# A two-layer graph attention kernel: the order of a few vector operations and of two loads

## The chip, the cores and the metric

The kernel runs on one core of a Trainium2 chip. A core has a TensorE (PE) for matrix products, a VectorE (DVE), a ScalarE (ACT) and a GpSimd (POOL) for the rest, and DMA queues that are fed here by SyncE (SP) and POOL. Every engine works through its own instructions in order and waits on semaphores for the others. The metric is the device time of one execution in microseconds (us), as the median of several.

## The reference

A graph attention network with two layers on 512 nodes of 768 features, then a residual sum and a layer norm:

```python
def gat_layer(x, W, a_s, a_d, b, edge_index, concat):
    n = x.shape[0]
    H, C = a_s.shape
    h = (x @ W).reshape(n, H, C)
    src, dst = (edge_index[0], edge_index[1])
    alpha_s = jnp.einsum('nhc,hc->nh', h, a_s)
    alpha_d = jnp.einsum('nhc,hc->nh', h, a_d)
    e = jax.nn.leaky_relu(alpha_s[src] + alpha_d[dst], NEG_SLOPE)
    m = jax.ops.segment_max(e, dst, num_segments=n)
    e = jnp.exp(e - m[dst])
    denom = jax.ops.segment_sum(e, dst, num_segments=n)
    alpha = e / (denom[dst] + EPS)
    msg = h[src] * alpha[:, :, None]
    out = jax.ops.segment_sum(msg, dst, num_segments=n)
    out = out.reshape(n, H * C) if concat else out.mean(axis=1)
    return out + b
...
h = gat_layer(x, W1, a_src1, a_dst1, b1, edge_list, concat=True)
h = jax.nn.elu(h)
out = gat_layer(h, W2, a_src2, a_dst2, b2, edge_list, concat=True)
...
x = _layernorm(x + _L0_gnn_ref(x, ...), axis=-1)
```

Layer 1 has 8 heads, each with a 768 x 768 slice of W1; layer 2 has one head, whose W2 has 8 x 768 rows. All data are float32. There are 16,896 edges with their self loops.

## The kernel before

The edges are turned once into a 512 x 512 matrix of counts (`cnt`, and `absent` where there is no edge), so that each head is dense: the features hs = x W1[h] (`projection`), the logits, the attention probabilities (`lift`, `leak`, `rank`, `weigh`, one block of 128 destinations each), their transpose PT, the aggregate of hs by PT with bias and elu (`mixed`, or `aggregate` and `elu`), whose transposed result gT is at once multiplied with W2's rows of this head (`second`) and added to layer 2's features h2. The loop over h (line 678) does the aggregate of head h, `second` of head h, the probabilities of head h + 1 and the projection of head h + 2. Layer 2 follows after the loop.

The three large products use a scheme of seven products of half matrices, P1 to P7, in the place of eight. It needs sums of quarters of both operands, which DVE makes: `left` (lines 228 to 231) of x or gT, `right` (L240, L241) of the weights, into t2 and t4, and for `mixed` `left_sums` (L586 to L589) of hs and `right_sums` (L597 to L600) of PT. A pair in `projection` or `second` is a multiplication on PE into a bank of PSUM and its evacuation by DVE or ACT; P2 adds to P1's bank, P4 to P7's and P3 to P5's, so PE may begin them only when the bank was evacuated. In `mixed` the products run P1, P6, P7, P2, P5, P4, P3 for three chunks c; P6 needs the second sum of PT (L598), P7 the third (L599), P4 the fourth (L600).

The program is written out by hand in the order in which each engine is to issue (`manual_schedule`); a planner doesn't reorder anything. Where a tile is used again, the framework adds the wait for the tile's last readers. Around the change:

- Head 1's projection runs over the start of the loop: `pairs[4]` to `pairs[13]`, each followed by the functions that `beside` lists for it. `give(t)` weighs a block of head 0's probabilities and sends it through DMA to be transposed (`turn_out`), `turn_in(t)` is an ACT copy of the landed block into PT (L553). `done[12]` and `pairs[13][1]` are the last two evacuations (L287). `some_logits` are two logit operations of head 1's block 2 (L257). `rsums` are the four sums of PT.
- `besides` goes to `mixed` of head 0 as the front of `fill`, a list of DVE operations with no hurry. `some(n)` issues n of them: one in the middle of each chunk, and at its end the rest of the list divided by the places still to come, rounded up.
- In the last turn of the loop (h = 6) the weight buffer "w2" gets W2's rows of head 7: a 576 KB piece into w2t1 (L103) and six row blocks of 384 KB (L109) from SP's queue, and from POOL's an adding transfer (L104), with a second one (L115, `last_sum`) later. Layer 2's vectors a_src2 and a_dst2, spread over 128 partitions, go into the buffers w2t2 and w2t4, which held the `right` sums of head 7's projection (L686). DVE multiplies W2's row blocks with them (L703, twelve operations into V), spread between the chunks c = 2 to 5 of head 6's aggregate, whose elu ends in L565.
- `second` evacuates P1 with L306 (L304 in head 0). `pairs[0][1]` and `pairs[1][1]` are the two halves of P1. `gsums[0]` to `gsums[3]` are gT's sums, L228 to L231. `spread` puts the logits of the next head through PE (L363), ahead of P2.

Of the kernel before, what the change touches and what calls it, by code (L numbers as in the profile page):

```python
# [36 lines left out]
def gat_pass(  # L37
# [19 lines left out]
    H = a_src1.shape[0]  # L57
# [40 lines left out]
    def load_w(W, h, slot, m):  # L98


        t1 = wpool.tile([P, HK, HALF], F32, name=f"{slot}t1")
        upper = m[:HK * P, :].rearrange("(k p) d -> p k d", p=P)
        nc.sync.dma_start(t1, upper[:, :, L])  # L103
        nc.gpsimd.dma_start(t1, upper[:, :, R], accum_op=ALU.add)  # L104
        W[h] = []
        for r in range(2):
            w = wpool.tile([P, HK, D], F32, name=f"{slot}{r}")
            for k in range(r * HK, (r + 1) * HK):
                nc.sync.dma_start(w[:, k - r * HK, :], m[k * P:(k + 1) * P, :])  # L109
            W[h].append(w)  # L110
        W[h].append(t1)

        def rest():

            nc.gpsimd.dma_start(W[h][0][:, :, R], m[HK * P:, R].rearrange("(k p) d -> p k d", p=P),  # L115
                                accum_op=ALU.add)
        return rest
# [4 lines left out]
    def load_w2(h, slot="w1"):  # L122
        return load_w(W2, h, slot, w2[h * D:(h + 1) * D, :])
# [99 lines left out]
    def left(aT, s):  # L223
        a11, a12 = aT[:, :HK, :HN], aT[:, HK:, :HN]
        a21, a22 = aT[:, :HK, HN:], aT[:, HK:, HN:]
        tt = nc.vector.tensor_tensor
        return dict(P1=a11, P2=a12, P3=s[:, 2], P4=a22, P5=s[:, 0], P6=s[:, 1], P7=a21), [
            lambda: tt(s[:, 0], a21, a22, op=ALU.subtract),  # L228
            lambda: tt(s[:, 1], s[:, 0], a11, op=ALU.subtract),
            lambda: tt(a21, a11, a21, op=ALU.subtract),  # L230
            lambda: tt(s[:, 2], a12, s[:, 1], op=ALU.add),  # L231
        ]
# [23 lines left out]
    def half_logits(h, t):  # L256
        return [lambda al=al, a=a, sign=sign: nc.vector.scalar_tensor_tensor(  # L257
            scr, HS[h][:, t, :], sign, a, op0=ALU.mult, op1=ALU.mult, accum_out=al[:, t:t + 1])
            for al, a, sign in zip(AL[h], A[h], (1.0, -1.0))]
# [138 lines left out]
    if not general:  # L398
# [5 lines left out]
        cps, done = {}, 0  # L404
# [49 lines left out]
        for n, batch in enumerate(batches):  # L454
# [9 lines left out]
            while pos < want:  # L464
                if pos == wholes:
                    pairs = projection(1, XA, B1)
# [19 lines left out]
    else:  # L486
# [16 lines left out]
        pairs = projection(1, XA, B1)  # L503
# [48 lines left out]
    def turn_in(t):  # L552
        nc.scalar.copy(PT.rearrange("p s n -> p (s n)").bitcast(U16).rearrange("p (s n h) -> p s n h", s=NT, h=2)[  # L553
            :, :, t * P:(t + 1) * P, :], parted.pop(t).rearrange("p (h s d) -> p s d h", h=2, s=NT))
# [24 lines left out]
    def left_sums(h):  # L579
        hs = HS[h]  # L580
        a11, a12, a21, a22 = hs[:, :2, L], hs[:, 2:, L], hs[:, :2, R], hs[:, 2:, R]
        s1, s2, s4 = (gS.rearrange("p a k n -> p a (k n)")[:, j, :].rearrange("p (k n) -> p k n", k=2)
                      for j in range(3))
        tt = nc.vector.tensor_tensor
        return dict(P1=a11, P2=a12, P3=s4, P4=a22, P5=s1, P6=s2, P7=a21), [
            lambda: tt(s1, a21, a22, op=ALU.subtract),  # L586
            lambda: tt(s2, s1, a11, op=ALU.subtract),
            lambda: tt(a21, a11, a21, op=ALU.subtract),
            lambda: tt(s4, a12, s2, op=ALU.add),  # L589
        ]  # L590
# [63 lines left out]
    AA, lsums = left_sums(0)  # L654
    BB, rsums = right_sums()
    some_logits = half_logits(1, 2)

    def give(t):
        weigh(q[t], t)
        turn_out(q[t], t)  # L660

    done = {n: (lambda n=n: pairs[n][1]()) for n in range(4, 13)}
    beside = {4: [lambda: give(0)], 5: [done[4]], 6: [done[5]], 7: [done[6], lambda: give(1)],
              8: [done[7], lambda: leak(q[3]), lambda: rank(q[3], 3), lambda: turn_in(0)], 9: [lambda: give(2), done[8]],
              10: [lambda: give(3), lambda: turn_in(1), done[9]], 11: [done[10], lsums[0]],
              12: [done[11], lambda: turn_in(2), *lsums[1:3]], 13: [done[12], some_logits[0], lambda: turn_in(3)]}
    for n in range(4, 14):
        pairs[n][0]()
        for f in beside[n]:
# [2 lines left out]
            load_w2(0)()  # L672
            B2, pending = right(W2[0], "w1")
    pairs[13][1]()
    for f in rsums:
        f()
    besides = [lsums[3], some_logits[1]]
    for h in range(H - 1):
        if h + 2 < H:
            load_w1(h + 2)()  # L680
        else:
            last_sum = load_w2(H - 1, "w2")
            A[H] = []
            for j, a in ((2, a_src2[0]), (4, a_dst2[0])):
                v = wpool.tile([P, HK, HALF], F32, name=f"w2t{j}").rearrange("p k n -> p (k n)")[:, :D]
                nc.sync.dma_start(v, row_bcast(a))  # L686
                A[H].append(v)
        GA, gsums = left(gT, gS)
        if h + 2 < H:
            finish = mixed(h, AA, BB, besides + [p for t in ((0, 1) if h else (0, 1, 3)) for p in half_logits(h + 1, t)])  # L690
        else:
            finish = []
            for c in range(DC):
                finish.append(aggregate(h, c))
                if c:
                    finish.pop(0)()
                if c < 2:
                    logits(h + 1, HS[h + 1], c)
                else:

                    for k in ((0, 1), (2,), (3,), (4, 5))[c - 2]:
                        for v, a, sign in zip(range(2), A[H], (1.0, -1.0)):
                            nc.vector.scalar_tensor_tensor(scr, W2[H - 1][k // HK][:, k % HK, :], sign, a,  # L703
                                                           op0=ALU.mult, op1=ALU.mult, accum_out=V[:, k, v:v + 1])
        besides = []
        if h + 2 < H:
            load_a(h + 2, a_src1[h + 2], a_dst1[h + 2])
        pairs = second(h, GA, B2)
        for m, _ in pairs[:2]:
            m()  # L710
        pairs[0][1]()
        for f in finish:
            f()
        gsums[0]()
        gsums[1]()
        pairs[1][1]()
        if pending:
            pending.pop(0)()
        spread(h + 1)
        pairs[2][0]()  # L720
        gsums[2]()
        pairs[3][0]()
        gsums[3]()
        if pending:
            pending.pop(0)()
        pairs[2][1]()
        pairs[3][1]()
        last = h + 2 == H
        q = [lift(h + 1, 0)]
        for n in range(2, 7):  # L730
            (m0, e0), (m1, e1) = pairs[2 * n:2 * n + 2]
            m0()
            if not last:
                m1()
            if n < 6:
                leak(q[n - 2])
                rank(q[n - 2], n - 2)
            if n < 5:
                q.append(lift(h + 1, n - 1))
            if last:  # L740

                if n > 3:
                    turn(q[n - 4], n - 4)
                if n == 6:
                    weigh(q[3], 3)
                m1(lambda: turn(q[3], 3) if n == 6 else None)
            if not last and n == 6:
                turn_in(0)
                weigh(q[2], 2)
                turn_out(q[2], 2)  # L750
            e0()
            if last and 2 < n < 6:
                weigh(q[n - 3], n - 3)
            if not last and 3 < n < 6:
                weigh(q[n - 4], n - 4)
                turn_out(q[n - 4], n - 4)
            if not last and n == 6:
                weigh(q[3], 3)
                turn_out(q[3], 3)
                load_w2(h + 1)()  # L760
            e1()
        if h + 2 < H:
            B_, sums = right(W1[h + 2], "w2")
            pairs = projection(h + 2, XA, B_)
            for n in range(14):
                pairs[n][0]()
                if n == 0:
                    turn_in(1)
                    B2, sums2 = right(W2[h + 1], "w1")
                if n in (1, 3):  # L770
                    sums[n // 2]()
                if n == 1:
                    AA, sums3 = left_sums(h + 1) if h + 3 < H else (None, [])
                pairs[n][1]()
                if n in (2, 4):
                    turn_in(1 + n // 2)
                if n == 5 and h + 3 < H:
                    BB, sums3 = right_sums()
                if 1 <= n < 9 and h + 3 < H:
                    sums3.pop(0)()  # L780
                if n in (9, 10):
                    sums2.pop(0)()
                if n in (11, 13):
                    logits(h + 2, HS[h + 2], 2 + (n - 11) // 2)
        else:
            last_sum()
            B2, sums2 = right(W2[H - 1], "w1")
# [35 lines left out]
    pairs = second(H - 1, GA, B2)  # L823
# [115 lines left out]
```

## Time and profile before

| | us |
|---|---|
| runs of the kernel before | 661.69, 660.57, 662.6; median 661.69 |
| the profiled execution, its own time | 662.61 |
| its span, first to last instruction | 660.8 |
| PE busy | 649.1 (98%) |
| DVE busy | 511.7 (77%) |
| ACT busy | 248.6 (38%) |
| POOL busy | 42.8 (6%) |
| DMA, mean over the span | 130 GB/s |

The page is of one execution. Times in the timeline are microseconds from the span's start: start, duration, engine, line, operation, output and inputs, shape, count; in brackets the idle time of the engine just before, and what ended it. Durations of neighbours overlap: a DVE operation starts before the one ahead of it is quite out of the pipe, so the distance from start to start is what an operation takes of its engine's time. On PE each product of `second` and `projection` is six instructions (1.94 us from start to start), each of `mixed` four (0.87 us).

### The profile page before, as it was taken

To read this page: it belongs to the slowest core of one execution; us is meant where nothing else is said; L and a number is where in the kernel's file an instruction comes from. 1 tells how busy PE (TensorE), PEld (TensorE's weight loads), DVE (VectorE), ACT (ScalarE), POOL (GpSimd) and SP (SyncE) were. 2 spreads that over 40 slices of the span, in tenths; PEclk is the share of its full clock that TensorE was granted. 3 is DMA by queue.
4 is the path that set the end of the run, shared out by engine and by line. 5 is a ranking of instruction groups with operands and counts; after the bars stand their busy time and mean duration, and the time that the engine had idled before them with its cause. 6 is when DMAs were issued, how large, how long until landed. Compare 5 with 4: busy or idle time off the path is not lost.

```text
span 660.8 us, 7107 instructions
## 1 busy us (share of the span) xinstructions
PE 649.1 (98%) x2419; PEld 401.1 (61%) x2419; DVE 511.7 (77%) x1102; ACT 248.6 (38%) x417; POOL 42.8 (6%) x52
## 2 busy tenths in 40 slices
PE   8999999999999999999999999999999999999995
PEld 4555567556865577556855586557755544644553
DVE  6979989977779587767688687868785579866785
ACT  2222646350635135440725035430735042333440
POOL 1300011010100110010000110011000000000000
PEclk9999999999999999999999999999999999999998
DMA  8801299177803882087605790196506674000122
GB/s 308 239 1 49 33 277 285 28 220 160 225 1 68 246 236 64 16 248 189 160 0 129 185 273 26 33 264 202 116 0 194 158 225 132 24 0 1 28 61 76
DMA packets 71355, 85.58 MB, mean 130 GB/s; under 512 B 36566, under 2 KB 55950, under 8 KB 71310
## 3 DMA queue, kind: packets, MB, share of 16 engines
q1 hardware_dynamic: 59022, 66.76, 32.2%
q0 software_dynamic: 12000, 17.70, 15.8%
q10 hardware_dynamic: 288, 0.59, 0.3%
q8 instruction: 21, 0.34, 0.2%
q14 instruction: 24, 0.20, 0.1%
HBM read 75.07 MB, written 1.57 MB: 116 GB/s over the span
## 4 chain that ended last, share of the span: by engine, by line
PE 93%; DMA 3%; DVE 2%; issue 1%; SPq 0%; ACT 0%; DVEq 0%
PE mm L248 61%; PE mm L625 17%; PE mm L352 5%; PE mm L571 3%; PE mm L891 3%; PE tr L430 2%; DMA w2t<-in_L_gnn_a_dst_dram 2%; DMA hs<-in_x_dram 1%; DVE scr L703 1%; PE bc L430 1%; PE bc L363 0%; DVE gT L565 0%; PE mm L327 0%; PE tr L819 0%; PE tr L540 0%
## 5 line engine op out<-in xcount | busy, mean ns | idle before, releaser
L248 PE MATMUL mm<-w,gT 128*128 128x384 f32 x288 | 97.8, 488 | 1.4 <-DVE u L306 1.4
L248 PE MATMUL mm<-w,xT 128*128 128x384 f32 x252 | 83.9, 487 | 0.0
L248 PEld LDWEIGHTS mm<-w,gT 128*128 128x128 f32 x288 | 53.4, 190 | 38.2 <-DVE u L306 3.9
L248 PEld LDWEIGHTS mm<-w,xT 128*128 128x128 f32 x252 | 47.7, 190 | 33.7 <-issue 0.4
L248 PE MATMUL mm<-w1t,gS 128*128 128x384 f32 x180 | 60.7, 486 | 0.0
L380 ACT ACTIVATE q<-q,nmax 128x512 f32<-128x512 f32 x36 | 25.8, 721 | 91.6 <-DVE nmax L378 91.6
L248 PE MATMUL mm<-w2t,xS 128*128 128x384 f32 x168 | 56.6, 487 | 0.0
L625 PE MATMUL mm<-PT,hs 128*128 128x256 f32 x216 | 52.5, 379 | 0.0
L629 ACT COPY u<-mm 128x256 f32<-128x256 f32 x18 | 6.7, 372 | 119.1 <-PE mm L625 119.1
L306 DVE TENSOR_TENSOR h<-h,mm 128x384 f32<-128x384 f32 x72 | 39.7, 551 | 13.9 <-PE mm L248 12.7
L248 PEld LDWEIGHTS mm<-w1t,gS 128*128 128x128 f32 x180 | 34.1, 190 | 23.6
L248 PEld LDWEIGHTS mm<-w2t,xS 128*128 128x128 f32 x168 | 31.8, 190 | 22.2 <-issue 0.2
L625 PEld LDWEIGHTS mm<-PT,hs 128*128 128x128 f32 x216 | 41.0, 190 | 6.9
L548 ACT COPY nr<-q 128x1024 uint16<-128x1024 uint16 x32 | 33.4, 1044 | 22.4 <-DVE q L534 15.5
L571 PE MATMUL mm<-PT,hs 128*128 128x512 f32 x96 | 41.6, 593 | 0.0
L418 DVE TENSOR_SCALAR os<-nodes,idx 128x512 bf16<-128x512 f16 x132 | 35.8, 343 | 4.1 <-PE tr L430 4.0
L625 PE MATMUL mm<-pS,gS 128*128 128x256 f32 x144 | 37.1, 380 | 1.1 <-DVE pS L598 1.1
L553 ACT COPY PT<-zr 128x1024 uint16<-128x1024 uint16 x32 | 37.1, 1159 | 2.0 <-DMA zr<-nr 2.0
L352 PE MATMUL mm<-w,xT 128*128 128x384 f32 x96 | 33.3, 493 | 0.0
L248 PE MATMUL mm<-w,gS 128*128 128x384 f32 x96 | 32.6, 486 | 0.0
L248 PE MATMUL mm<-w1t,gT 128*128 128x384 f32 x96 | 32.5, 487 | 0.0
L571 PEld LDWEIGHTS mm<-PT,hs 128*128 128x128 f32 x96 | 18.2, 190 | 22.9 <-issue 21.5
(158 smaller groups left out, 1030.2 us busy)
## 6 DMA issues: line engine op xcount, KB each, us to landing
w<-in_L_gnn_W_dram SPq DMA_DIRECT2D x90, 384.0 KB, 6.1
w<-in_L_gnn_W_dram POOLq DMA_DIRECT2D x15, 576.0 KB, 8.9
w2t<-in_L_gnn_W_dram SPq DMA_DIRECT2D x8, 576.0 KB, 4.7
w2t<-in_L_gnn_W_dram POOLq DMA_DIRECT2D x8, 576.0 KB, 8.8
w1t<-in_L_gnn_W_dram SPq DMA_DIRECT2D x7, 576.0 KB, 4.5
w1t<-in_L_gnn_W_dram POOLq DMA_DIRECT2D x7, 576.0 KB, 9.4
a_s<-in_L_gnn_a_src_dram SPq DMA_DIRECT2D x8, 384.0 KB, 3.5
a_d<-in_L_gnn_a_dst_dram SPq DMA_DIRECT2D x8, 384.0 KB, 3.4
```

The lines of the kernel that those rows point to most:

```text
L248: nc.tensor.matmul(ps[:, :HALF], A_[p][:, k, i * P:(i + 1) * P], B_[p][:, k, :], start=start and k == 0, stop=k == HK - 1, skip_group_chec ...
L306: nc.vector.tensor_tensor(a, a, ps, op=ALU.subtract if p == "P7" else ALU.add)
L352: nc.tensor.matmul(ps, xT[:, r * HK + k, t * P:(t + 1) * P], W1[h][r][:, k, cols], start=r == 0 and k == 0, stop=r == 1 and k == HK - 1)
L380: nc.scalar.activation(q, q, AF.Exp, bias=nmax, scale=-1.0)
L418: nc.vector.tensor_scalar(hot[c], nodes, idx[:, 1, c:c + 1], None, op0=ALU.is_equal)
L430: nc.tensor.matmul(cps[t][r:r + B, :N], od[:, c, k * B:(k + 1) * B], hot[c], start=todo[b] == hits[b], stop=todo[b] == 1, tile_position=(0 ...
L548: nc.scalar.copy(apart.rearrange("p (h n) -> p h n", h=2), q.bitcast(U16).rearrange("p (n h) -> p h n", h=2))
L553: nc.scalar.copy(PT.rearrange("p s n -> p (s n)").bitcast(U16).rearrange("p (s n h) -> p s n h", s=NT, h=2)[:, :, t * P:(t + 1) * P, :], p ...
L571: nc.tensor.matmul(ps[:, :N], HS[h][:, s, c * P:(c + 1) * P], PT[:, s, :], start=(s == 0), stop=(s == NT - 1))
L625: nc.tensor.matmul(bank[p][:, :HN], A_[p][:, k, c * P:(c + 1) * P], B_[p][:, k, :], start=over is None and k == 0, stop=k == 1, skip_group ...
L629: nc.scalar.copy(u, part("P1"))
L891: nc.tensor.matmul(ps[:, :cols.stop - cols.start], PT[:, s, t * P:(t + 1) * P], h2[:, s, cols], start=(s == 2), stop=(s == 1))
```

## The change

Three edits of order. The same operations and transfers are issued, but for their places:

1. In `beside[13]`, `some_logits[0]` leaves, and the first two sums of PT (`rsums[:2]`, L597 and L598) come in behind `turn_in(3)`, ahead of `pairs[13][1]`. The other two sums stay behind it. Both logits now go to `besides`.
2. In the last turn of the loop the vectors a_src2 and a_dst2 are loaded ahead of W2's rows of head 7 (`load_w2`).
3. In `second` of heads 0 to 6, the evacuation `pairs[1][1]` moves from behind `gsums[1]` to ahead of it. Layer 2's last `second` (lines 836 to 838) keeps its order.

```diff
-              12: [done[11], lambda: turn_in(2), *lsums[1:3]], 13: [done[12], some_logits[0], lambda: turn_in(3)]}
+              12: [done[11], lambda: turn_in(2), *lsums[1:3]], 13: [done[12], lambda: turn_in(3), *rsums[:2]]}
...
     pairs[13][1]()
-    for f in rsums:
+    for f in rsums[2:]:
         f()
-    besides = [lsums[3], some_logits[1]]
+    besides = [lsums[3], *some_logits]
...
         else:
-            last_sum = load_w2(H - 1, "w2")
             A[H] = []
             for j, a in ((2, a_src2[0]), (4, a_dst2[0])):
                 v = wpool.tile([P, HK, HALF], F32, name=f"w2t{j}").rearrange("p k n -> p (k n)")[:, :D]
                 nc.sync.dma_start(v, row_bcast(a))
                 A[H].append(v)
+            last_sum = load_w2(H - 1, "w2")
...
         gsums[0]()
+        pairs[1][1]()
         gsums[1]()
-        pairs[1][1]()
```

## The prediction

> **What bounds the kernel.** The page comes first, its busy shares and its chain that ended last:
>
> ```profile
> PE 649.1 (98%) x2419; PEld 401.1 (61%) x2419; DVE 511.7 (77%) x1102; ACT 248.6 (38%) x417; POOL 42.8 (6%) x52
> PE 93%; DMA 3%; DVE 2%; issue 1%; SPq 0%; ACT 0%; DVEq 0%
> ```
>
> TensorE does the work and ends last for 93%. Only the places where PE stands still can pay, so the chain in order of time is next. It leaves PE twice in the middle of the kernel:
>
> ```profile
> 89.16 0.56 DVE hs L287
> 89.72 0.61 DVE pS L597
> 90.35 0.70 DVE pS L598
> 91.10 18.04 PE mm L625 x80
> ...
> 530.69 10.58 DMA w2t<-in_L_gnn_a_dst_dram
> ...
> 556.85 0.47 DVE u L306
> 557.37 11.88 PE mm L248 x36
> ```
>
> From 91.10 to 528.90 and from 557.37 to 652 the chain is PE alone. The timeline, all engines, around the first place:
>
> ```profile
> 87.51 1.17 ACT L553 COPY PT<-zr 128x1024 uint16<-128x1024 uint16 x1 [0.65 <-DMA zr<-nr]
> 87.97 0.95 DVE L257 SCALAR_TENSOR_TENSOR scr<-hs,a_s 128x768 bf16<-128x768 f32 x1
> 89.16 0.56 DVE L287 TENSOR_TENSOR hs<-mm,hs 128x384 f32<-128x384 f32 x1 [0.24 <-PE mm L248]
> 91.10 1.13 PE L625 MATMUL mm<-pS,gS 128*128 128x256 f32 x4 [1.11 <-DVE pS L598]
> ```
>
> PE waits 1.11 us for the second probability sum (L598), which stood behind a logit (L257) and an evacuation (L287). And around the second:
>
> ```profile
> 539.89 0.96 DVE L703 SCALAR_TENSOR_TENSOR scr<-w,w2t 128x768 bf16<-128x768 f32 x1 [1.61 <-DMA w2t<-in_L_gnn_a_src_dram]
> 541.37 0.96 DVE L703 SCALAR_TENSOR_TENSOR scr<-w,w2t 128x768 bf16<-128x768 f32 x1 [0.52 <-DMA w2t<-in_L_gnn_a_dst_dram]
> 547.23 0.63 ACT L564 ACTIVATE nr<-nr 128x512 f32<-128x512 f32 x1
> 549.22 0.69 DVE L565 SCALAR_TENSOR_TENSOR gT<-nr,zr 128x512 f32<-128x512 f32 x1
> 554.32 2.20 PE L248 MATMUL mm<-w,gT 128*128 128x384 f32 x6 [0.54 <-DVE u L306]
> 557.37 2.20 PE L248 MATMUL mm<-w,gT 128*128 128x384 f32 x6 [0.85 <-DVE u L306]
> ```
>
> DVE idles 1.61 and 0.52 us for the two layer-2 vectors, is then busy without a hole, and so reaches both P1 evacuations (L306) late.
>
> **Part 1, the two sums in head 0.** L257 leaves the place at 87.97. L597 reads all of PT, so it now waits for ACT's last turn_in, 87.51 + 1.17 = 88.68, and starts at 88.71 (ACT to DVE takes 0.03: L564 ends at 534.18, L565 starts at 534.21). DVE is in order: behind it stand the last evacuation and the other sums. L598 starts 0.71 later (90.35 - 89.64), 89.42, and ends at 90.11; PE follows after 0.06 (91.04 to 91.10), so P6 starts at 90.17 instead of 91.10. What is late next is the third sum: L287 starts 0.61 after L598, at 90.03, L599 0.48 after that and ends at 91.19; P7 starts at 91.25. A product whose start waited takes 0.97 (91.10 to 92.07), any other 0.87, so P2 starts at 92.22 instead of 92.94: **0.72 us** earlier. All of `mixed` hangs on PE from there.
>
> The logit doesn't vanish; `besides` gets it. Nine pieces instead of eight go through `some`: 1+2, 1+2, 1+2 instead of 1+2, 1+2, 1+1. The extra one therefore falls behind the last L644 (109.17), ahead of head 0's P1 evacuation (L304 at 111.11, which had 0.64 us of idle time before it). With PE 0.72 ahead: L644 at 108.45, logits at 108.80 and 109.80, the evacuation 0.88 after, 110.68. That is 0.43 ahead, not 0.72. From there DVE has no slack up to 124.85; its one hole (0.43 us at 122.95, for ACT's q) comes from its own chain. There it meets PE:
>
> ```profile
> 124.30 0.55 DVE L304 TENSOR_SCALAR h<-mm 128x384 f32<-128x384 f32 x1
> 124.90 4.14 PE L248 MATMUL mm<-w1t,gT 128*128 128x384 f32 x12
> ```
>
> P7 ends at 121.03 + 3.87 = 124.90 and P4 needs the evacuation that ends at 124.85. Afterwards PE is there at 124.18, but the evacuation ends at 124.42, or at 124.31 with the 0.11 of part 3. With 0.06 for the handover P4 starts at 124.37: **0.54 us** of the 0.72 are left. Later DVE idles again (3.79 us before L283 at 146.56), so nothing more is lost. The moved logits also release a_s 2 us later (109.8 for 107.6); head 2's vectors, 3.5 us of transfer, are not used until after 160, so that costs nothing.
>
> **Part 3, one evacuation between gT's sums.** L228 to L229 takes 0.99 (554.90 to 555.89) because the second reads the first; to an independent operation 0.88. The order L228, L306, L229 takes 0.88 + 0.46 + 0.88 = 2.22 for 0.99 + 0.88 + 0.46 = 2.33, so DVE gains 0.11. The Trainium skill, "VectorE: DVE Perf Modes", The DRAIN you can't avoid, says that the flush comes after every operation and chaining costs the same: by it the 0.11 would be 0 and part 1 worth 0.43. I take the rows. L229 itself goes 0.35 us later; P6 (2 us on) still finds it. In heads 1 to 5 PE shows no gap here, only weight loads that wait 0.3 us under a running matmul, so those are worth 0. It pays in heads 0 and 6.
>
> **Part 2, the vectors ahead of the last W2.** Two issues of 0.43 us move ahead of seven on SP's queue, no POOL transfer moves. Their buffers w2t2 and w2t4 are free when PE is through head 7's P6 (513.2) and P4 (521.0). SP stands idle from 508.3 to 525.03, where it waits for w2t1, so the second vector may hold it till 521.0 and nothing behind is late: the W2 issues start at 525.03 as before. The vectors take 9.6 us behind W2; alone 3.5 (the page's a_s row). The skill's "DMA: Bandwidth & Descriptors", [...] Either way they are there by 525, and L703 asks at 538.2. The same page (Issuing engines are not separate DMA queues) speaks against the move: all queues share 16 engines, so the first vector now takes room from W2[6]. The windows show 239 and 205 GB/s at full share between 513.3 and 519; 0.39 MB at 205 is 1.9 us. W2[6]'s t1 sum (issued 509.53, landing after 9.4, 518.9) is read at 521.63: covered with 0.8 to spare, and a further 1.2 before P3 at 524.83 would notice. I take 0.
>
> DVE then goes on at 538.20 (rows 0 to 2 of W2, issued by 527, land in about 6). Four L703 (1.0 each, the last 0.88) to 542.08; gT 0.60; two to 544.56; gT; two to 547.04. There gT waits for ACT until 547.89 (547.23 + 0.63 + 0.03) instead of 549.22: 1.33 of the 2.13 us remain. Then 0.60 and four L703: the first P1 evacuation at 552.37 (before 553.71), ending at 552.92. PE is through the spread at 553.60, so its 0.54 wait is gone. L565 at 552.84, L228 at 553.56, the second evacuation (part 3) at 554.44 to 554.99; PE wants it at 555.54: the 0.85 is gone too. Head 0 shows the same stretch without waits: spread at 112.85, P6 at 117.16, 4.31 us. Here it took 553.17 to 559.40, 6.23. **Gain 1.92 us** (0.54, 0.85 and what weight loads and starts lose around each). Without part 3 the second evacuation would end at 556.0: 1.3. Without part 2, 1.0. Downstream the first P6 evacuation is DVE-late by 0.3 and catches up in the 1.38 us hole before 563.48.
>
> **The sum.** 0.54 + 1.92 = 2.46 us, 0.37%. The profiled execution took 662.61 us (span 660.8), so that one would take 660.15. The median of the runs is 661.69; from it, **659.2 us**. What a measurement can tell from no change is about 0.3%, 2.0 us.
>
> **Rivals.**
> *Head 0 gives all back* (0.14). DVE's chain to P4 is at its end there already; if the extra logit costs it 0.5 more than I counted, only 1.92 is left: 659.8. For it: PE's 0.1 us loss at 124.90. Against: the 0.64 us hole.
> *W2's rows take the vectors' place* (0.10). L703 also reads W2[7]; if rows land near 540, DVE waits anyway, part 2 is worth nothing, part 3 about 1.0: 1.5 in all, 660.2. For it: t1, rows and sum share one busy stretch of DMA to 538. Against: the vectors stood last in that queue.
> *Head 0 keeps all 0.72* (0.08), if DVE runs tighter: 659.0.
> *Slower* (0.06). The first vector's transfer delays W2[6]'s sum, the DVE add at 521.63 stands ahead of the evacuations that PE's P3 needs. Covered to 518.9 + 3.9 us; beyond that each us is paid in full. It takes 6.4 us of delay to undo the gain and over 8.3 for slower by 0.3%: say 664. My estimate is 1.9, so little speaks for it.
> *As summed*: 0.62.
>
> **Chances.** With a scatter of 1 us (runs of 660.57 to 662.6), as summed passes 0.3% in 85 of 100, the 659.0 case in 90, the 659.8 case in 45, the 660.2 case in 10: faster 0.67, slower 0.06, same 0.27. The range: down from 659.0 by the scatter, 657.9; up from 660.2 by 0.7, 660.9.
>
> **What would show it.** P6 of head 0 near 90.2 and P7 with a short wait of its own behind L599; two L257 in a row at 109; P4 near 124.4, behind DVE; no L703 waiting on a DMA, L565 waiting for ACT near 547.3; no PE wait on L306 in head 6, its P6 near 556.9. Wrong would be: a DVE wait for W2 rows before L703, a wait of the add at 521.63, or a PE gap after 124.

## The result, and the profile after

The changed kernel takes **660.29 us** (median of 20 runs, 659.46 to 661.12), the kernel before 661.58 us (20 runs, 660.57 to 662.6). The ratio is 0.9981, 95% interval 0.9974 to 0.9988, which is 1.26 us (0.8 to 1.7) of the 661.58. It is faster, but by half of what was forecast, and inside the band of 0.3% in which the prediction had put 0.27 of its chance.

The page of the changed kernel (its execution took 660.2 us, span 658.4), busy shares and the chain that ended last:

```profile
PE 649.1 (99%) x2419; PEld 402.0 (61%) x2419; DVE 511.2 (78%) x1102; ACT 248.7 (38%) x417; POOL 42.4 (6%) x52
PE 95%; DVE 3%; ACT 0%; DMA 0%; issue 0%; DVEq 0%; ACTq 0%
```

PE's work is the same 649.1 us in a span 2.4 us shorter. The chain in order of time (start, length, what), at the two places:

```profile
88.45 0.70 DVE pS L597
89.18 0.70 DVE pS L598
89.93 1.13 PE mm L625 x4
91.08 17.14 PE mm L625 x76
...
552.58 0.44 PE bc L363 x4
553.01 13.55 PE mm L248 x42
```

In head 6 the chain no longer leaves PE. The timeline of the changed kernel, head 0 first, then head 6:

```profile
88.45 0.69 DVE L597 TENSOR_TENSOR pS<-PT 128x512 f32<-128x512 f32 x1 [0.68 <-ACT PT L553]
89.93 1.13 PE L625 MATMUL mm<-pS,gS 128*128 128x256 f32 x4 [0.22 <-DVE pS L598]
109.59 0.96 DVE L257 SCALAR_TENSOR_TENSOR scr<-hs,a_d 128x768 bf16<-128x768 f32 x1
110.48 0.55 DVE L304 TENSOR_SCALAR u<-mm 128x384 f32<-128x384 f32 x1
124.14 4.14 PE L248 MATMUL mm<-w1t,gT 128*128 128x384 f32 x12
...
537.44 0.95 DVE L703 SCALAR_TENSOR_TENSOR scr<-w,w2t 128x768 bf16<-128x768 f32 x1
547.13 0.69 DVE L565 SCALAR_TENSOR_TENSOR gT<-nr,zr 128x512 f32<-128x512 f32 x1 [0.76 <-ACT nr L564]
552.41 0.60 PE L363 MATMUL bc<-ident,al_s 128*128 128x128 f32 x4
552.85 4.04 PE L248 MATMUL mm<-w,gT 128*128 128x384 f32 x12
556.72 4.03 PE L248 MATMUL mm<-w1t,gS 128*128 128x384 f32 x12
```

The lines show PE's wait for L598 down from 1.11 us to 0.22, L597 waiting for ACT in its place, the extra logit right ahead of head 0's first P1 evacuation (L304), and in head 6 no wait of L703 for a DMA and none of PE for L306.

This fits the forecast closely, and that is the puzzle: between the two profiled executions the change is worth all of the 2.4 us, between the medians 1.3.

Three distances on PE make the traces comparable, since the start of the work moves from execution to execution. They are read from the PE timeline of each kernel: from the first P3 product of head 1's projection (85.09 before, 84.81 after) to P4 of head 0 and to head 6's aggregate (its first product at 528.70 before, 527.94 after), and in head 6 from `spread` (L363) to P6. All in us; the fourth column is the idle time that L703 spent on the vectors.

| kernel | P3 to P4, head 0 | P3 to head 6 | L703 idle | spread to P6, head 6 |
|---|---|---|---|---|
| before, the page shown | 39.81 | 443.61 | 2.13 | 6.23 |
| before again, three executions | 39.82, 39.82, 39.81 | 443.62, 443.63, 443.62 | 1.03, 0.89, 0.78 | 5.05, 4.91, 4.89 |
| part 1 alone | 39.41 | 443.21 | 0.58 | 4.90 |
| part 2 alone | 39.81 | 443.61 | 0 | 4.90 |
| part 3 alone | 39.81 | 443.51 | 0.77 | 4.31 |
| parts 2 and 3 | 39.80 | 443.50 | 0 | 4.31 |
| all three (the change) | 39.33 | 443.13 | 0 | 4.31 |
| before, padded | 39.81 | 443.61 | 3.58 | 8.27 |
| the change, padded | 39.35 | 443.15 | 0 | 4.31 |
| the change, P2 copies on ACT | 39.15 | 442.85 | 0 | 4.31 |

### The profile page after: what moved, and what is told of

It reads as the page before. It is cut to its first block, busy times and chain, and to the rows that moved or that the text cites. A ratio compares the mean times of both kernels' runs of the same rounds, so it can differ in the third digit from the quotient of the medians.

```text
span 658.4 us, 7115 instructions
## 1 busy us (share of the span) xinstructions
PE 649.1 (99%) x2419; PEld 402.0 (61%) x2419; DVE 511.2 (78%) x1102; ACT 248.7 (38%) x417; POOL 42.4 (6%) x52
## 4 chain that ended last, share of the span: by engine, by line
PE 95%; DVE 3%; ACT 0%; DMA 0%; issue 0%; DVEq 0%; ACTq 0%
PE mm L248 59%; PE mm L625 17%; PE mm L571 6%; PE mm L352 5%; PE mm L891 3%; PE tr L430 2%; PE bc L154 1%; PE bc L430 1%; PE bc L363 1%; DMA zr<-nr 0%; DVE q L373 0%; DVE q L378 0%; DVE q L528 0%; PE mm L327 0%; PE tr L819 0%
## 5 line engine op out<-in xcount | busy, mean ns | idle before, releaser
L306 DVE TENSOR_TENSOR h<-h,mm 128x384 f32<-128x384 f32 x72 | 39.6, 551 | 14.4 <-PE mm L248 13.8
```

Of the source, the lines that this page charges most:

```text
L306: nc.vector.tensor_tensor(a, a, ps, op=ALU.subtract if p == "P7" else ALU.add)
```

## The experiments

Two theories stood against each other. A: the page of before shows the usual stall, and the 1.1 us between traces and medians is lost elsewhere. B: that page shows an execution whose stall in head 6 was longer than usual.

**The kernel before, again.** No edit.

> The kernel before, once more, for a second profile of it. Theory A (the traces are typical: the change is worth 2.4 us and the medians' 1.3 us differ by what happens elsewhere): the new profile shows the same stall in head 6, the vectors landing near 541, L703 idle for 2.1 us, TensorE waiting 0.54 and 0.85 us for L306, 6.2 us from the spread to P6. Theory B (the profile of before showed an execution with a stall longer than usual): the span is about 1 us shorter and the stretch from the spread to P6 takes nearer 5.2 us, because the vectors land sooner. Ratio 1.000 by both.

Measured: 661.67 us, ratio 0.9998 (0.9989 to 1.0007). The timeline of its profile in head 6, DVE and PE:

```profile
538.64 0.95 DVE L703 SCALAR_TENSOR_TENSOR scr<-w,w2t 128x768 bf16<-128x768 f32 x1
540.64 0.96 DVE L703 SCALAR_TENSOR_TENSOR scr<-w,w2t 128x768 bf16<-128x768 f32 x1 [1.03 <-DMA w2t<-in_L_gnn_a_dst_dram]
553.62 0.60 PE L363 MATMUL bc<-ident,al_s 128*128 128x128 f32 x4
554.06 2.10 PE L248 MATMUL mm<-w,gT 128*128 128x384 f32 x6
556.63 2.20 PE L248 MATMUL mm<-w,gT 128*128 128x384 f32 x6 [0.47 <-DVE u L306]
558.67 4.03 PE L248 MATMUL mm<-w1t,gS 128*128 128x384 f32 x12
```

The first vector is there when L703 asks for it; only the second is late, by 1.03 us. The first P1 evacuation costs PE nothing, the second 0.47. The stretch takes 5.05 us instead of 6.23, as theory B said. The span is 660.3 us, shorter by 0.5 and not by the expected 1, since the work began 0.44 us later (P3 at 85.53 instead of 85.09). Two more executions, also without an edit, ask how usual that is:

> The kernel before, a third look at its head 6. Theory B: the second vector keeps DVE about 0.6 to 1.1 us in all, the stretch from the spread to P6 takes 4.9 to 5.1 us as in the second profile. Theory A: 2.1 us and 6.2.

> The kernel before, a fourth look, with the same numbers: 4.9 to 5.1 us by theory B, 6.2 by theory A. A mixture of both would say that the landing of the vectors simply varies from execution to execution.

Measured: 661.45 and 660.68 us; stretches of 4.91 and 4.89, with 0.89 and 0.78 us of idle L703. With part 1 alone and part 3 alone, where the vectors also stand behind W2, that makes six executions: the first vector lands 7.3 to 7.8 us after its issue in five of them, and 9.6 us after it on the page of before. Theory A falls. The five were taken on three chips; which chip the page of before comes from is not known, so whether the late landing belongs to that one execution or to its chip is not shown.

**Part 1 alone.**

```diff
-... 13: [done[12], some_logits[0], lambda: turn_in(3)]}
+... 13: [done[12], lambda: turn_in(3), *rsums[:2]]}
-    for f in rsums:
+    for f in rsums[2:]:
-    besides = [lsums[3], some_logits[1]]
+    besides = [lsums[3], *some_logits]
```

> Part 1 alone, the two sums ahead. Theory A: L598's wait falls from 1.11 us to about 0.2, TensorE is 0.62 us ahead in mixed and 0.4 us ahead from head 0's P4 on, since the extra logit holds the vector engine back (0.48 less the 0.11 of part 3); ratio 0.9994. Theory B says the same of this part. A rival, that part 1 loses all of it again by P4: ratio 1.000, P4 no earlier than before relative to the first products.

Measured: 661.55 us, ratio 1.0 (0.9991 to 1.0008). The time can't tell 0.4 us from nothing. The trace can: `mixed` runs 0.67 us earlier (first product of `second` at 23.21 from P3, before 23.88 to 23.89), and from P4 on 0.40 is left, as theory and sum had it. The rival, that all of it is given back, falls.

**Part 2 alone, and parts 2 and 3.**

```diff
-            last_sum = load_w2(H - 1, "w2")
             A[H] = []
...
                 A[H].append(v)
+            last_sum = load_w2(H - 1, "w2")
```

> Part 2 alone, the vectors ahead of the last W2. Theory A: no L703 waits for a DMA, the wait of 0.54 us before P2 is gone, the second L306 still ends after TensorE is ready, with a wait of about 0.5 us; 1.3 us saved, ratio 0.998. Theory B: the same trace, but the ratio 0.9990 or nearer to 1, since the stall that it removes is usually shorter.

Measured: 661.53 us, ratio 0.9995 (0.9986 to 1.0003). PE's timeline:

```profile
553.60 0.60 PE L363 MATMUL bc<-ident,al_s 128*128 128x128 f32 x4
554.04 2.10 PE L248 MATMUL mm<-w,gT 128*128 128x384 f32 x6
556.46 2.20 PE L248 MATMUL mm<-w,gT 128*128 128x384 f32 x6 [0.32 <-DVE u L306]
558.50 4.03 PE L248 MATMUL mm<-w1t,gS 128*128 128x384 f32 x12
```

4.90 us with the vectors there in time, and 4.89 to 5.05 in the three new executions without the edit: in the usual execution part 2 alone buys at most 0.15 us.

> Parts 2 and 3 without part 1. Theory A: 1.92 us saved, ratio 0.9971, from the spread to P6 in head 6 takes 4.3 us. Theory B: the same 4.3 us in the trace, but 0.8 us saved, ratio 0.9988.

Measured: 660.85 us, ratio 0.9987 (0.9979 to 0.9996), as theory B said; the stretch takes 4.31, and head 0 gains 0.11 from part 3 (443.50).

**Part 3 alone.**

```diff
         gsums[0]()
+        pairs[1][1]()
         gsums[1]()
-        pairs[1][1]()
```

> Part 3 alone, the vectors still behind W2. Theory B (the usual stall in head 6 is the one of the second profile, 0.74 us over the 4.31 of an undisturbed stretch, and mostly the second L306): the stretch from the spread to P6 takes 4.3 to 4.5 us, so part 3 alone takes nearly all of it, and in head 0 P4's gate moves 0.11 us; ratio 0.9989. Theory A (the stall of the first profile): the stretch takes 5.2, ratio 0.998.

Measured: 660.79 us, ratio 0.999 (0.9978 to 1.0003). DVE and PE in head 6:

```profile
539.89 0.96 DVE L703 SCALAR_TENSOR_TENSOR scr<-w,w2t 128x768 bf16<-128x768 f32 x1 [0.77 <-DMA w2t<-in_L_gnn_a_dst_dram]
553.14 0.60 PE L363 MATMUL bc<-ident,al_s 128*128 128x128 f32 x4
553.57 4.04 PE L248 MATMUL mm<-w,gT 128*128 128x384 f32 x12
557.45 4.03 PE L248 MATMUL mm<-w1t,gS 128*128 128x384 f32 x12
```

L703 still waits for the second vector, and PE doesn't stand still at all: 4.31 us. With the usual landing this one moved line does all that the change does in head 6. In head 0 the 0.11 us are there (443.51), but not where they were expected: without part 1, P4 starts no earlier (39.81). It is P4 itself that takes 3.87 us to the start of P5 instead of 3.98: the evacuation ahead of it ends earlier, and PE loads P4's first weights 0.12 us ahead of its first product (124.85 and 124.97) instead of together with it (124.90).

**The landing made later, with and without part 2.** Two transfers of a vector's size into pS, which nobody reads any more by then:

```diff
             last_sum = load_w2(H - 1, "w2")
+            for j in range(2):
+                nc.sync.dma_start(pS.rearrange("p a k n -> p (a k n)")[:, j * D:(j + 1) * D], row_bcast(a_src2[0]))
```

> The kernel before with two more transfers of a vector's size put between W2's rows and the layer-2 vectors, into a buffer that nobody reads any more. If the landing of the vectors sets the stall, they land 2.5 to 3.5 us later (0.79 MB at 230 to 300 GB/s) and the stretch from the spread to P6 grows from about 5.1 us by the whole of it, to about 8; ratio 1.004. If the stall is the vector engine's own work, the stretch stays near 5.

> The changed kernel with the same two transfers behind W2's rows, where the vectors are no longer behind them. If only the vectors' place counts: the stretch stays at 4.31 us, ratio to the kernel before 0.998 as without the pad. If the traffic itself hurts (W2's rows or the adding transfer late): a wait of L703 or of a later product, ratio nearer 1.

Measured: 664.63 us, ratio 1.0045 (1.003 to 1.0061) for before; 660.06 us, ratio 0.9977 (0.9967 to 0.9986) for the changed kernel. The timeline of the padded kernel before, DVE and PE (L705 is L703, two lines down):

```profile
542.18 0.96 DVE L705 SCALAR_TENSOR_TENSOR scr<-w,w2t 128x768 bf16<-128x768 f32 x1 [3.58 <-DMA w2t<-in_L_gnn_a_src_dram]
556.13 5.80 PE L248 MATMUL mm<-w,gT 128*128 128x384 f32 x12 [2.04 <-DVE u L306]
558.58 0.55 DVE L306 TENSOR_TENSOR u<-u,mm 128x384 f32<-128x384 f32 x1
561.77 1.45 PE L248 MATMUL mm<-w1t,gS 128*128 128x384 f32 x4
```

Its windows around the pause (start and end, length, busy time of PE, PEld, DVE, ACT and POOL with counts, then the granted clock, the DMA share and GB/s):

```profile
553.50:556.00 2.50, 0.59 (x5) 0.35 (x3) 2.43 (x8) 0.69 (x1) 0.00 (x0) 1.00 1.12 244
556.00:558.00 2.00, 1.87 (x3) 1.18 (x4) 1.93 (x4) 0.00 (x0) 0.00 (x0) 0.53 1.06 353
558.00:560.00 2.00, 2.00 (x5) 1.05 (x4) 2.00 (x4) 0.00 (x0) 0.00 (x0) 0.62 0.40 158
```

The landing of the vectors sets the stall: 3.58 us of idle L703 make a stretch of 8.27, and with the vectors ahead of W2 the same traffic costs nothing. Of the 3.96 us above an undisturbed 4.31, 2.19 are the late start of P2 and 1.77 the longer time that its instructions take. The windows show a lowered clock there, but the 1.77 are not all its cost: at the full clock the second half of P2 would have had to wait for the second L306 (558.58). On the page of before that half starts 0.61 us after the second L306, and P6 2.03 after that. Counted so, P6 would have started at 561.22 instead of 561.77 at the full clock; by this estimate the clock cost about 0.55. So part 2 is insurance: it removes the dependence on a landing, which was late on the page of before and usually isn't.

**Head 0's P2 copies on ACT.** The changed kernel, with this in `second`:

```diff
-                if new and (h == 0 or h == H - 1 and p == "P1"):
+                if new and h == 0 and p == "P2":
+                    nc.scalar.copy(a, ps)
+                elif new and (h == 0 or h == H - 1 and p == "P1"):
```

> The changed kernel with head 0's two P2 evacuations (a copy, L304) on the scalar engine instead of the vector engine. If the vector engine's chain is what gives back part of the sums' gain at P4 of head 0: P4 starts 39.2 us after the last projection product (39.33 in the changed kernel, 39.81 before) without its wait, the whole 0.6 us is kept, ratio 0.9979. If something else holds P4, it stays at 39.33.

Measured: 660.18 us, ratio 0.9982 (0.9973 to 0.9991), not to be told from the change itself in time. In the trace P4 starts at 39.15 and DVE reaches its evacuation with room:

```profile
123.03 0.55 DVE L306 TENSOR_SCALAR h<-mm 128x384 f32<-128x384 f32 x1
124.40 4.03 PE L248 MATMUL mm<-w1t,gT 128*128 128x384 f32 x12
```

It ends at 123.58, 0.82 us ahead of P4 (L306 is L304 here). What gave back part of the sums' gain was DVE's chain to this evacuation, and 0.28 us more are kept (442.85 for 443.13): 0.18 at P4's start and the rest within P4, as in part 3 alone.

## Why the prediction was right, and where its size was wrong

The direction, the range and the mechanisms held; the time of 659.2 us was 1.1 too low, because one term of the sum was read from an unusual execution. For part 3, these are DVE's lines around gT's sums in head 0, before and then in the changed kernel:

```profile
112.64 0.96 DVE L228 TENSOR_TENSOR gS<-gT 128x768 f32<-128x768 f32 x1
113.63 0.96 DVE L229 TENSOR_TENSOR gS<-gS,gT 128x768 f32<-128x768 f32 x1
114.51 0.55 DVE L304 TENSOR_SCALAR u<-mm 128x384 f32<-128x384 f32 x1
114.97 1.35 DVE L240 TENSOR_TENSOR w1t<-w1t,w 128x1152 f32<-128x1152 f32 x1
...
112.00 0.96 DVE L228 TENSOR_TENSOR gS<-gT 128x768 f32<-128x768 f32 x1
112.88 0.55 DVE L304 TENSOR_SCALAR u<-mm 128x384 f32<-128x384 f32 x1
113.34 0.95 DVE L229 TENSOR_TENSOR gS<-gS,gT 128x768 f32<-128x768 f32 x1
114.21 1.35 DVE L240 TENSOR_TENSOR w1t<-w1t,w 128x1152 f32<-128x1152 f32 x1
```

By its steps:

- **Part 1.** L597 was to wait for ACT and start 0.03 after it: ACT ended at 88.42, L597 started at 88.45. P6 was to be 0.93 earlier, and is 0.89 (5.12 from P3 instead of 6.01). `mixed` was to gain 0.72, and gains 0.64: L597 to L598 took 0.73, and P7 started 0.14 after L599's end where I had counted 0.06. The two logits in a row, the late evacuation and P4 behind DVE are there; 0.54 was to be left and **0.48** is.
- **Part 3.** The order L228, L304, L229 takes 2.21 us from L228 to L240 (112.00 to 114.21), before 2.33. On PE that is worth 0.11 us in head 0 without part 1 (443.61 to 443.50 with parts 2 and 3) and 0.08 with it (443.21 to 443.13). The rows decided against the rule that the prediction had set beside them, from "VectorE: DVE Perf Modes", The DRAIN you can't avoid. That section measured a chain of copies with a semaphore after each and with one at the end, at the same time; it times no pair in which the second operation reads what the first wrote, as L229 reads L228's sum here.
- **Part 2.** The issue at 512.66 and 520.40, W2's start unmoved, W2[6]'s sum still read on time (L240 at 520.88, right behind L285), L703 without a wait, L565 then waiting for ACT: all as worked out. The objection from "DMA: Bandwidth & Descriptors", Issuing engines are not separate DMA queues, made no difference that any wait shows, with the pad neither.
- **The step that was mis-sized is "Gain 1.92 us".** The subtraction 6.23 - 4.31 is right for the execution on the page: from P3 to head 6's P6 the two profiled executions differ by 2.40 us, which is 0.48 and 1.92. But 6.23 is one landing of a transfer. The other executions give 4.89 to 5.05, so the term measures **0.58 to 0.74**, and with head 0's 0.48 the change is worth 1.06 to 1.22 us, inside the measured 0.8 to 1.7. Within the term it is part 2 that was too large: without part 3 the shown execution would have gained 1.3, as the prediction says, the usual one 0 to 0.15. What part 3 adds to part 2 was right: 0.6 (1.92 less 1.3) by the prediction, 0.59 (4.90 less 4.31) in the runs.

There was a sign of it that I passed by. The profiled execution took 662.61 us, 0.92 more than the median, and was the slowest of the three runs shown. I subtracted the gain read from it from the median of all three, as if they all had the same stall. And the unknown that I bounded, the 9.6 us of the vector's landing, was bounded only for the new place, not for the old.

That 660.29 lies in the range is in part luck. The summed 659.2 with its scatter of 1 us would have ended at 660.2; the range reached to 660.9 for the sake of the rival at 660.2, which named nearly the measured time with the wrong mechanism, since W2's rows were there when L703 asked.

## What to carry to other kernels

A wait for a DMA is one draw; here L703's wait for the vectors was 2.13, 1.03, 0.89 and 0.78 us in four executions of one kernel. A wait for an engine in a fixed order repeated: PE's wait for L598 was 1.11 us in all eight profiled executions that keep the old order there. Before a gain is read off a DMA wait, take a second profile of the same kernel. The profiled execution's own time is only a hint: a surplus over the median can also come from a later start of the work, as the 662.11 us of the second profile show, whose stretch took 5.05. When two edits remove the same stall from two sides, cost each at the usual arrival as well: here one moved evacuation was enough, and the loads ahead only make the result independent of the landing.

## What the runs showed of the hardware

- The landing of one and the same transfer, with the same bytes ahead of it in its queue, took from 7.3 to 9.6 us. Why it was late on the page of before is open; no run tells it.
- The first 0.8 to 0.9 us of L703's wait cost nothing, since the next chunk waits for ACT anyway (0.76 us at 547.13 in the changed kernel): idle times of 0, 0.58, 0.78 and 0.89 us all give 4.89 to 4.91. Beyond, 1.03 gives 5.05 and 2.13 gives 6.23.
- In the padded kernel a PE pause of 2.04 us was followed by a granted clock of 0.53 and 0.62 in the two windows shown above (weight loads 0.64 us apart until 559.5, instead of 0.32), and the twelve instructions of P2 took 5.64 us instead of 3.87. Of the 1.77 more, about 0.55 is the clock's by the estimate above. The pauses of 0.54, 0.85 and 1.11 us in the kernel before left the clock at 1.00 (windows of 549 to 562, 20 to 100). The Trainium skill, "TensorE: Matmul & The Clock Gate", Part 1, asks for an idle window of about 3.4 us before the clock drops; here a pause of 2.04 was enough, with only the four short products of `spread` in the 0.6 us ahead of it and PE busy without a gap before them.
- The start of the work moved by 1.4 us among twelve executions of kernels that are the same up to there (P3 of head 1's projection at 84.25 to 85.61), more than what the change is worth.
